# Graph network kernel: gathered pairs tied to the products beside them, the count matrix moved in four pieces a group, 56 edge slots a node

## The chip, the cores and the metric

The kernel runs on one core of one Trainium2 chip. The metric is device microseconds of one execution; the time before is the median of three runs.

## What is computed

A graph has 2500 nodes with 256 features and 80000 edges, sorted by their target. The features are normalized and passed through a relu, then go through three edge convolutions and a last linear layer over all four feature sets:

```python
def _edge_conv(x, src, dst, W, b):
    xi = x[dst]
    xj = x[src]
    m = jnp.concatenate([xi, xj - xi], axis=-1) @ W + b
    s = jax.ops.segment_sum(m, dst, num_segments=N)
    cnt = jax.ops.segment_sum(jnp.ones((dst.shape[0],), m.dtype), dst, num_segments=N)
    return s / jnp.maximum(cnt, 1.0)[:, None]
...
for W, b in ((W0, b0), (W1, b1), (W2, b2)):
    h = jax.nn.relu(_edge_conv(h, src, dst, W, b))
    xs.append(h)
return jnp.concatenate(xs, axis=-1) @ Wf + bf
```

The result is added to the input `x`.

## The kernel before

The sum over edges is a product with a count matrix: entry (m, n) says how many edges go from node m to node n. All nodes are cut into 20 tiles of 128. Of each layer the kernel first makes z, the node features times the lower half of the weights (`nodes_split`, L754, 20 tiles; layer 0 has its own steps for it), keeps it in SBUF as a high and a low part (`zh`, `zl`), and stores it to DRAM as `z_dram`. In `layer` (L934) it then multiplies z with the count matrix: for each of 20 source tiles four products (two column halves, high and low), and four products of the features with the upper half of the weights (L953). Each such step of the generator is a unit; there are 24 in a group.

The targets are worked off in groups of columns. The last 2388 nodes are in windows of 6 nodes; 80 windows (480 columns) make a group, so there are five groups, the last with 78 windows (468 columns). Two tiles `a` hold two groups of the count matrix at a time. In layer 0 the matrix of group g + 1 is built from the edges (`build`, L838) while group g is multiplied, and `finish` (L850) stores the built group to DRAM (`a_dram`) with one transfer. Layer 1 runs through the groups from 4 down to 0 and layer 2 from 0 up to 4; the two groups that lie in SBUF at a layer's start are used first, and the other three are loaded by `load_a` (L856), each with one transfer, when a tile comes free (L1089).

The first 112 nodes (FEW) are not in the count matrix. Each has EDGES slots for edges (L330), and row numbers in `who` say which row of `z_dram` each slot wants; unused slots point to a row of zeros. For layer 0 `gather` (L874) issues one indirect transfer a slot on POOL, the transfers of slots 8 to 59 adding into eight partial sums in SBUF, which `add_sums` (L882) folds on DVE at the layer's end. `layer_few` (L923) multiplies them in; the next layer's `nodes_split` stands behind it on PE. For layers 1 and 2 `gather_pairs` (L904) gathers two slots at a time into one of four rooms, and DVE adds a pair to a running sum before its room is used again. It starts with four pairs and then does a step at units 1, 5, 9, 13, 17 and 21 of each group (the loop at L1056). `final` (L778) adds the features' share of the last linear layer, tile by tile, at the start of each group.

Wrappers whose name ends in "o" (PEo, DVEo, POOLo, ACTo, SPo; the helper is L280) fix an instruction behind everything written earlier for its engine. Instructions on plain PE, ACT and SP may be placed earlier by the scheduler when their inputs are ready. The stores of `z_dram` in `nodes_split` (L764) are on SPo; the loads and stores of the count matrix are on plain SP. A count of nodes with more edges than slots (`shares`, with `most`) sets a flag that makes a general kernel run afterwards.

Of the kernel before, what the change touches and what calls it, by code (L numbers as in the profile page):

```python
# [8 lines left out]
F32 = mybir.dt.float32  # L9
# [302 lines left out]
def by_windows(ctx: ExitStack, tc: tile.TileContext, x, src, dst, Ws, bs, Wf, bf, out, missing):  # L312
    nc = tc.nc
    PE, DVE, ACT, POOL, SP = nc.tensor, nc.vector, nc.scalar, nc.gpsimd, nc.sync
    PEo, DVEo, POOLo, ACTo, SPo = (InOrder(tc, e) for e in (PE, DVE, POOL, ACT, SP))
    P = 128
    N, D = x.shape
    E = src.shape[0]
    NT = (N + P - 1) // P
# [7 lines left out]
    S = 8  # L327
    CAP = CH * P
    FEW = 112
    EDGES = 60  # L330
    SUMS = 8
    PAIRS = 4
    NW = (N - FEW) // W
# [14 lines left out]
    NG = len(GWS)  # L348
# [20 lines left out]
    def bank():  # L369
        return ps[-1].tile([P, 512], F32, name="bank")  # L370
# [3 lines left out]
    hT = const.tile([P, DC, NP], F32, name="hT")  # L374
    zh = const.tile([P, NT, D], F32R, name="zh")
    zl = const.tile([P, NT, D], F32R, name="zl")
# [19 lines left out]
    z_dram = [dram.tile([NP, D], F32, name=f"z_dram{l}") for l in range(L)]  # L396
    who = const.tile([P, EDGES], I32, name="who")
    sums = const.tile([P, SUMS, D], F32, name="sums")
# [4 lines left out]
    a_dram = [dram.tile([P, NT, n * W], F32, name=f"a_dram{g}") for g, n in enumerate(GWS)]  # L403
# [25 lines left out]
    ws = [None] * L  # L429
# [6 lines left out]
    def load_wt(l, queue=SP):  # L436
        queue.dma_start(ws[l][0], Ws[l][0:D, :].rearrange("(c p) d -> p c d", p=P))
# [41 lines left out]
    POOL.memset(mine[:IN_LAST], 1.0)  # L479
    POOL.memset(most, float(EDGES))  # L480
    POOL.memset(most[:IN_LAST], float(CAP))
# [104 lines left out]
    def few_edges():  # L586

        es, ed = edges[WG - 1]
        own = pp.tile([P, EDGES], I32, name="own")
        POOLo.tensor_scalar(who, es[:, :EDGES], -NONE, None, op0=OP.add)  # L590
        POOLo.tensor_scalar(own, away[:, WG - 1, :EDGES], 0.0, None, op0=OP.is_equal)
        POOLo.tensor_tensor(who, who, own, op=OP.mult)
# [161 lines left out]
    def nodes_split(l, t, zf):  # L754
        pz = bank()
        for c in range(DC):
            PE.matmul(pz[:, :D], hT[:, c, t * P:(t + 1) * P], ws[l][1][:, c, :],  # L757
                      start=(c == 0), stop=(c == DC - 1))
        sc = share[:, t:t + 1]
        if t == NT - 1:  # L760
            DVEo.scalar_tensor_tensor(zf, pz[:, :D], sc, brow[:, l % 2, :], op0=OP.mult, op1=OP.add)
        else:
            ACT.activation(zf, pz[:, :D], AF.Copy, scale=sc)
        SPo.dma_start(z_dram[l][t * P:(t + 1) * P, :], zf)  # L764
        DVEo.tensor_copy(zh[:, t, :], zf)
        DVEo.tensor_sub(zl[:, t, :], zf, zh[:, t, :].bitcast(F32))
# [22 lines left out]
    def group_of(g):  # L789
        return FEW + sum(GWS[:g]) * W, GWS[g] * W  # L790

    def touched(g):
        c0, n = group_of(g)
        return [t for t in range(NT) if (t + 1) * P > c0 and t * P < c0 + n]

    def new_a(g):

        n = group_of(g)[1]
        a = apools[g % 2].tile([P, NT * GS], F32R, name="a")
        return a[:, :NT * n].rearrange("p (t n) -> p t n", n=n)  # L800
# [49 lines left out]
    def finish(g, a):  # L850
        c0, n = group_of(g)
        ACTo.copy(a[PAD:PAD + 1, NT - 1, :n], cnt[PAD:PAD + 1, c0:c0 + n])
        SP.dma_start(a_dram[g], a.bitcast(F32))
        yield

    def load_a(g):  # L856
        a = new_a(g)
        SP.dma_start(a.bitcast(F32), a_dram[g])
        return a

    def by_count(g):
# [12 lines left out]
    def gather(l):  # L874

        for e in range(EDGES):
            POOLo.indirect_dma_start(
# [9 lines left out]
    def room():  # L887

        return hot.tile([P, BW * CH, P], BF16, name="one_m", bufs=AHEAD).rearrange(
            "p k m -> p (k m)").bitcast(F32).rearrange("p (i d) -> p i d", i=2)  # L890

    def rooms(l):

        for _ in range(AHEAD):
            two = room()
            yield two[:, 0, :]
            yield two[:, 1, :]
        for i in range(SUMS):
            yield sums[:, i, :]
        for _ in range(AHEAD):  # L900
            yield hot.tile([P, BW * CH, NB], BF16, name="one_n", bufs=AHEAD).rearrange(
                "p k m -> p (k m)")[:, :2 * D].bitcast(F32)

    def gather_pairs(l):  # L904

        got = []
        for k in range(EDGES // 2 + PAIRS):
            if k >= PAIRS:
                if k == PAIRS + 1:
                    DVEo.tensor_add(sums[:, :2, :], got[0], got[1])  # L910
                elif k > PAIRS:
                    DVEo.tensor_add(sums[:, :2, :], sums[:, :2, :], got[k - PAIRS])
            if k < EDGES // 2:
                two = room()
                got.append(two)
                for i in range(2):
                    POOLo.indirect_dma_start(
                        out=two[:, i, :], out_offset=None, in_=z_dram[l][:, :],
                        in_offset=bass.IndirectOffsetOnAxis(ap=who[:, 2 * k + i:2 * k + i + 1], axis=0))
            if k >= PAIRS - 1:  # L920
                yield

    def layer_few(l):  # L923
        pa = ps_agg.tile([P, DC, 512], F32, name="pa")
        for o in range(DC):
            for c in range(DC):
                PEo.matmul(pa[:, o, :FEW], ws[l][0][:, c, o * P:(o + 1) * P], hT[:, c, :FEW],
                           start=(c == 0), stop=False)
            for z in (zh, zl):
                PEo.matmul(pa[:, o, :FEW], z[:, NT - 1, o * P:(o + 1) * P], cnt_few, start=False, stop=False)  # L930
            PEo.matmul(pa[:, o, :FEW], sums[:, 0, o * P:(o + 1) * P], only, start=False, stop=True)
        ACTo.activation(hT[:, :, :FEW], pa[:, :, :FEW], AF.Relu)

    def layer(l, g, a, own, PE=PE, ACT=ACT):  # L934

        c0, n = group_of(g)
        pa = ps_agg.tile([P, DC, 512], F32, name="pa")
        ways = [(o, c) for o in range(DC) for c in range(DC)]
        units = [(0, k) for k in range(NT)]
        for i, u in enumerate(own):  # L940
            units.insert(u + i, (1, i))
        last = {}
        for kind, i in units:
            last.update({o: (kind, i, o) for o in (range(DC) if kind == 0 else ways[i][:1])})
        for kind, i in units:
            if kind == 0:
                for o in range(DC):
                    for z in (zh, zl):
                        PE.matmul(pa[:, o, :n], z[:, i, o * P:(o + 1) * P], a[:, i, :n],  # L949
                                  start=(i == 0 and z is zh), stop=(z is zl and last[o] == (kind, i, o)))  # L950
            else:
                o, c = ways[i]
                PE.matmul(pa[:, o, :n], ws[l][0][:, c, o * P:(o + 1) * P], hT[:, c, c0:c0 + n],  # L953
                          start=False, stop=(last[o] == (kind, i, o)))
            yield
        ACT.activation(hT[:, :, c0:c0 + n], pa[:, :, :n], AF.Relu)  # L956

# [7 lines left out]
    a = new_a(0)  # L965
# [55 lines left out]
    for g in range(NG):  # L1021
# [26 lines left out]
        if g + 1 < NG:  # L1048
            run(finish(g + 1, a1))
            held, a = a, a1  # L1050
# [4 lines left out]
    tiles = {NG - 1: a, NG - 2: held}  # L1055
    for l in range(1, L):  # L1056
        groups = list(range(NG))
        if l % 2:
            groups.reverse()


        last = [t for t in touched(groups[0]) if t]
        for t, zf in zip([t for t in range(1, NT) if t not in last] + last + [0], rooms(l)):
            nodes_split(l, t, zf)
        few = gather_pairs(l)
        next(few)
        if l + 1 < L:
            load_b(l + 1)
            load_wb(l + 1)
            load_wt(l + 1)  # L1070
        finished = []
        for j, g in enumerate(groups):
            now = [t for t in touched(g) if t not in finished]
            for t in now:
                final(l, t)
            finished += now
            rest = add_rest(now) if l == 1 else None
            if j == NG - 1:
                load_wf(l + 1)
            for u, _ in enumerate(layer(l, g, tiles[g], LATE)):  # L1080
                if u % 4 == 1:
                    next(few, None)
                if rest and u in (1, NT):
                    next(rest, None)
            if j == 1 and l + 1 < L:
                DVEo.tensor_sub(ws[l + 1][0], ws[l + 1][0], ws[l + 1][1])
            if j + 2 < NG:
                del tiles[g]
                tiles[groups[j + 2]] = load_a(groups[j + 2])  # L1089
        run(few)  # L1090
        add_sums(2)
        layer_few(l)
# [41 lines left out]
```

## Time and profile before

| | us |
|---|---|
| median of three runs | 531.79 (531.63 to 532.43) |
| the profiled execution, its own time | 533.3 |
| its span, first to last instruction | 531.6 |
| TensorE products busy in the span | 506.9 |
| POOL busy | 268.9 |
| DVE busy | 264.6 |

PE is TensorE's products, PEld its weight loads, DVE is VectorE, ACT ScalarE, POOL GpSimd and SP the queue that issues most transfers. Times in the views are counted from the first instruction. The profile gives the granted clock of TensorE and, by engine, what ended each wait. "issue" is time in which an engine waited for nothing that the profile shows. Layer 0 ends near 216, layer 1 near 360 and layer 2 near 508.

### The profile page before, as it was taken

The numbers are of one execution on the slowest core, as the hardware profiler recorded it, in microseconds if no ns is written. First come the engines' busy times: TensorE is split into PE (matmuls) and PEld (weight loads), VectorE is DVE, ScalarE is ACT, GpSimd is POOL, SyncE is SP. The second block draws the span as 40 slices with busy tenths as digits, with TensorE's granted clock in tenths as the row PEclk, the third lists the DMA queues.
The fourth block names the chain that finished last, engine by engine and source line by source line (L and its number), as shares of the span: only waits on it lengthen the run. The fifth ranks groups of instructions, "written<-read, shape, count | busy, mean of one in ns | idle before, by whom it ended". The sixth has DMA issues, their size and how long they took to land.

```text
span 531.6 us, 7489 instructions
## 1 busy us (share of the span) xinstructions
PE 506.9 (95%) x2875; PEld 414.1 (78%) x2875; DVE 264.6 (50%) x556; ACT 136.0 (26%) x310; POOL 268.9 (51%) x243
## 2 busy tenths in 40 slices
PE   8999999999999993999899999999996999999995
PEld 4898887888787882888587878878883878787884
DVE  7999888888888501582134140426620313303133
ACT  5676666746443400330000000005200000000000
POOL 3793257888888850007856462720273537354000
PEclk9999999999999998799999999999997999999998
DMA  8238749988968586343499999883334868998323
GB/s 275 82 99 137 142 144 355 391 164 268 222 168 291 82 320 129 98 141 91 107 415 331 234 276 244 114 108 118 110 105 142 351 238 255 193 283 92 30 89 110
DMA packets 37683, 100.29 MB, mean 189 GB/s; under 512 B 4663, under 2 KB 31750, under 8 KB 36230
## 3 DMA queue, kind: packets, MB, share of 16 engines
q0 software_dynamic: 19264, 29.84, 34.8%
q1 hardware_dynamic: 17446, 68.78, 33.4%
q10 hardware_dynamic: 928, 1.11, 0.7%
q8 instruction: 24, 0.39, 0.3%
q14 instruction: 21, 0.17, 0.1%
HBM read 62.21 MB, written 37.50 MB: 188 GB/s over the span
## 4 chain that ended last, share of the span: by engine, by line
PE 66%; POOL 14%; DMA 14%; issue 4%; DVE 1%; ACT 0%; SPq 0%; POOLq 0%; ACTq 0%
PE pa L949 33%; POOL sums L280 14%; PE bank L781 10%; DMA sums<-z_dram,who 10%; PE bank L757 7%; PE pa L953 6%; PE pz L280 6%; PE bank L280 2%; DMA wf<-in_L_gnn_Wf_dram 2%; PE pa L280 1%; DMA z_dram<-zl 1%; DMA z_dram<-zh 1%; DMA dst_i<-in_dst_dram 1%; PE turned L280 1%; DVE sums L280 0%
## 5 line engine op out<-in xcount | busy, mean ns | idle before, releaser
L280 POOL DMA_INDIRECT one_m<-z_dram,who x120 | 121.1, 1009 | 168.8 <-DVE sums L280 53.3
L949 PE MATMUL pa<-a,zh 128*128 128x480 f32 (+1 forms) x400 | 153.9, 385 | 0.3 <-issue 0.3
L949 PE MATMUL pa<-a,zl 128*128 128x480 f32 (+1 forms) x400 | 151.9, 380 | 0.3 <-issue 0.3
L280 POOL DMA_INDIRECT sums<-z_dram,who x60 | 104.2, 1737 | 24.7 <-issue 17.4
L280 DVE TENSOR_TENSOR sums<-sums,one_m 128x512 f32<-128x512 f32 x56 | 38.8, 692 | 103.3 <-DMA one_m<-z_dram,who 99.6
L949 PEld LDWEIGHTS pa<-a,zl 128*128 128x128 f32 x400 | 75.1, 188 | 13.2 <-issue 1.2
L949 PEld LDWEIGHTS pa<-a,zh 128*128 128x128 f32 x400 | 75.1, 188 | 12.8 <-issue 0.5
L280 PE MATMUL pa<-a,zh 128*128 128x480 f32 (+1 forms) x200 | 81.6, 408 | 0.0
L280 DVE TENSOR_TENSOR one_m<-iota_m,key_m 128x1024 bf16<-128x1024 bf16 x100 | 68.8, 688 | 17.6 <-PE bank L280 15.3
L280 PE MATMUL pa<-a,zl 128*128 128x480 f32 (+1 forms) x200 | 75.7, 379 | 0.0
L956 ACT ACTIVATE hT<-pa 128x960 f32<-128x960 f32 (+1 forms) x10 | 9.7, 968 | 243.8 <-PE pa L953 212.1
L280 DVE SCALAR_TENSOR_TENSOR acc<-bank,share,acc 128x256 f32<-128x256 f32 x60 | 28.5, 483 | 79.6 <-PE bank L781 69.0
L280 ACT CAST a<-bank 128x480 fp32r<-128x480 f32 x100 | 51.0, 566 | 59.7 <-PE bank L280 55.1
L280 DVE TENSOR_TENSOR one_n<-iota_n,key_n 128x960 bf16<-128x960 bf16 x100 | 65.3, 653 | 0.0
L781 PE MATMUL bank<-wf,hT 128*128 128x256 f32 x240 | 56.3, 391 | 2.0 <-issue 1.5
L781 PEld LDWEIGHTS bank<-wf,hT 128*128 128x128 f32 x240 | 47.1, 197 | 12.3 <-issue 5.3
L280 PEld LDWEIGHTS <-one_m 128*128 128x128 bf16 x796 | 43.3, 98 | 8.9 <-issue 3.3
L280 PE MATMUL bank<-one_n,one_m 128*128 128x120 bf16 x796 | 49.0, 216 | 0.2 <-DVE one_n L280 0.2
L280 PEld LDWEIGHTS pa<-a,zh 128*128 128x128 f32 x200 | 37.7, 188 | 8.5 <-issue 3.0
L280 PEld LDWEIGHTS pa<-a,zl 128*128 128x128 f32 x200 | 37.6, 188 | 7.0 <-issue 2.1
L953 PE MATMUL pa<-hT,wt 128*128 128x480 f32 (+1 forms) x80 | 35.4, 573 | 4.6 <-issue 4.5
L757 PE MATMUL bank<-wb,hT 128*128 128x256 f32 x160 | 36.0, 388 | 0.0
(145 smaller groups left out, 417.2 us busy)
## 6 DMA issues: line engine op xcount, KB each, us to landing
a<-a_dram SPq DMA_DIRECT2D x5, 4800.0 KB
a_dram<-a SPq DMA_DIRECT2D x4, 4800.0 KB
a_dram<-a SPq DMA_DIRECT2D x1, 4680.0 KB
a<-a_dram SPq DMA_DIRECT2D x1, 4680.0 KB
out_dram<-acc SPq DMA_DIRECT2D x19, 128.0 KB
z_dram<-one_m SPq DMA_DIRECT2D x16, 128.0 KB
z_dram<-sums SPq DMA_DIRECT2D x16, 128.0 KB
acc<-in_x_dram POOLq DMA_DIRECT2D x4, 512.0 KB
```

Of the source, the lines that this page charges most:

```text
L280: return self.tc.keep_in_program_order(call(*args, **kwargs))
L757: PE.matmul(pz[:, :D], hT[:, c, t * P:(t + 1) * P], ws[l][1][:, c, :], start=(c == 0), stop=(c == DC - 1))
L781: PE.matmul(po[:, :D], hT[:, c, t * P:(t + 1) * P], wfs[l][:, c, :], start=(c == 0), stop=(c == DC - 1))
L949: PE.matmul(pa[:, o, :n], z[:, i, o * P:(o + 1) * P], a[:, i, :n], start=(i == 0 and z is zh), stop=(z is zl and last[o] == (kind, i, o)))
L953: PE.matmul(pa[:, o, :n], ws[l][0][:, c, o * P:(o + 1) * P], hT[:, c, c0:c0 + n], start=False, stop=(last[o] == (kind, i, o)))
L956: ACT.activation(hT[:, :, c0:c0 + n], pa[:, :, :n], AF.Relu)
```

## The change

The number of edge slots falls from 60 to 56. The stores and loads of the count matrix are made in four transfers of five source tiles each. The store of the last group leaves `finish` and is written after the node products of layer 1 (the second of the three layers, `l == 1`), on plain SP. `layer` remembers its latest product in `unit`, and from the fifth pair on the first gather of each pair waits for the product that was the latest when it was written.

```diff
-    EDGES = 60
+    EDGES = 56
...
     def finish(g, a):
         c0, n = group_of(g)
         ACTo.copy(a[PAD:PAD + 1, NT - 1, :n], cnt[PAD:PAD + 1, c0:c0 + n])
-        SP.dma_start(a_dram[g], a.bitcast(F32))
+        if g + 1 < NG:
+            store_a(g, a)
         yield
+
+    def store_a(g, a):
+        for t in range(0, NT, 5):
+            SP.dma_start(a_dram[g][:, t:t + 5, :], a[:, t:t + 5, :].bitcast(F32))
 
     def load_a(g):
         a = new_a(g)
-        SP.dma_start(a.bitcast(F32), a_dram[g])
+        for t in range(0, NT, 5):
+            SP.dma_start(a[:, t:t + 5, :].bitcast(F32), a_dram[g][:, t:t + 5, :])
         return a
...
                 for i in range(2):
-                    POOLo.indirect_dma_start(
+                    d = POOLo.indirect_dma_start(
                         out=two[:, i, :], out_offset=None, in_=z_dram[l][:, :],
                         in_offset=bass.IndirectOffsetOnAxis(ap=who[:, 2 * k + i:2 * k + i + 1], axis=0))
+                    if k >= PAIRS and i == 0:
+
+                        tc.add_manual_dep(d.ins, unit[0].ins.name, mybir.DependencyInfo(
+                            mybir.DependencyClass.Sync, mybir.DependencyReason.DATA), reason="spread over the layer")
...
+    unit = [None]
...
-                        PE.matmul(pa[:, o, :n], z[:, i, o * P:(o + 1) * P], a[:, i, :n],
-                                  start=(i == 0 and z is zh), stop=(z is zl and last[o] == (kind, i, o)))
+                        unit[0] = PE.matmul(pa[:, o, :n], z[:, i, o * P:(o + 1) * P], a[:, i, :n],
+                                            start=(i == 0 and z is zh),
+                                            stop=(z is zl and last[o] == (kind, i, o)))
             else:
                 o, c = ways[i]
-                PE.matmul(pa[:, o, :n], ws[l][0][:, c, o * P:(o + 1) * P], hT[:, c, c0:c0 + n],
-                          start=False, stop=(last[o] == (kind, i, o)))
+                unit[0] = PE.matmul(pa[:, o, :n], ws[l][0][:, c, o * P:(o + 1) * P], hT[:, c, c0:c0 + n],
+                                    start=False, stop=(last[o] == (kind, i, o)))
...
             nodes_split(l, t, zf)
+        if l == 1:
+
+            store_a(NG - 1, tiles[NG - 1])
         few = gather_pairs(l)
```

## The prediction

> **What bounds the kernel now.** I read the page's busy table and its row of granted clock, then the chain of work that ended last, the table of waits, and windows around the places where TensorE (PE) stops.
>
> ```profile
> span 531.6 us, 7489 instructions
> ...
> PE 506.9 (95%) x2875; PEld 414.1 (78%) x2875; DVE 264.6 (50%) x556; ACT 136.0 (26%) x310; POOL 268.9 (51%) x243
> ...
> PEclk9999999999999998799999999999997999999998
> ```
>
> PE is busy for all but 24.7 us. The first dip of the clock is the end of layer 0. The chain there (start, duration, what):
>
> ```profile
> 191.35 0.30 issue
> 191.66 1.54 POOL sums L280
> 193.20 0.30 issue
> 193.50 17.73 DMA sums<-z_dram,who
> ...
> 213.72 2.47 PE pa L280 x10
> 216.19 18.36 PE bank L757 x80
> ...
> 358.14 1.77 PE pa L280 x16
> 359.91 17.28 PE bank L757 x80
> ```
>
> It leaves PE and runs through the 60 accumulating gathers: POOL issues one every 1.84 us (1.54 + 0.30), the last lands 17.73 us after its issue, VectorE (DVE) folds the eight partial sums from 211.26 to 213.67, and only then PE ends the product of the first 112 nodes. The last two lines are the same two stages a layer later, undisturbed. The waits agree:
>
> ```profile
> DVE sums L280 <- DMA sums<-z_dram,who: 25.6, 1, 25.6
> PE pa L280 <- DVE sums L280: 9.1, 1, 9.1
> ```
>
> Windows there (busy time of PE, PEld, DVE, ACT, POOL; granted clock, DMA share, GB/s):
>
> ```profile
> 176.00:180.00 4.00, 4.00 (x38) 3.46 (x37) 3.27 (x10) 1.57 (x3) 3.39 (x3) 1.00 0.62 84
> 192.00:196.00 4.00, 4.00 (x21) 3.56 (x19) 0.00 (x0) 0.00 (x0) 2.74 (x2) 1.00 0.92 375
> 208.00:212.00 4.00, 0.00 (x0) 0.00 (x0) 0.74 (x1) 0.00 (x0) 0.00 (x0) 0.50 0.43 51
> ```
>
> From 189 to 204 the DMA engines carry the store of the last group (375 GB/s) over the gathers; then PE idles and its clock halves. The second dip, in the first group of layer 2, is another kind of stop:
>
> ```profile
> 403.50 0.56 PE L953 MATMUL pa<-hT,wt 128*128 128x480 f32 x1 [0.84 <-issue]
> 404.92 0.56 PE L953 MATMUL pa<-hT,wt 128*128 128x480 f32 x1 [0.85 <-issue]
> ```
>
> PE waits for no engine, yet takes an instruction only each 0.70 us (weight load, product, weight load). From 399.08 to the next group's first product at 414.23 pass 15.15 us; the group after needs 3.22 + 3.45 = 6.67 for the same work, so 8.5 us are lost. A short one in layer 1 (255.87 to 264.56, 8.69 against 3.14 + 3.45) loses 2.1.
>
> **What the Trainium skill says.** "DMA: Bandwidth & Descriptors", Queues, rings and completion order: an engine round-robins between the queues it has work for and changes only after a whole packet. The trace agrees: during that store an engine alternates one packet of 37,440 bytes (1.40 us) with one gathered row of 1,024 bytes (0.10 us). The same page, Anatomy of one DMA: a semaphore wait is held on the issuing sequencer, so a gated gather holds up POOL, not the DMA engines; no gate is in this trace. "TensorE: Matmul & The Clock Gate", Part 1: an idle array falls to half clock and must be busy a while to come back. Here the clock is 0.50 for 10.2 us, from 208.0. "Runtime: NRT & Kernel Launch", Instruction fetch mechanics, describes instructions streamed in 16 KiB blocks, mostly hidden; 24 packets of 16,384 bytes are in the trace, but neither page nor trace gives the cause of the 0.70 us pace.
>
> **Part by part.**
>
> *56 edges.* Four gathers fewer in layer 0: 4 x 1.84 = 7.4 us of POOL, so the last one is issued at about 186.1, not 193.5. In layers 1 and 2 two pairs fewer each, beside the products: nothing on the path. The largest number of edges into one of the first 112 nodes in these inputs is 47, so the flag for the general kernel stays down.
>
> *Four transfers a group.* 11 transfers (5 stores, 6 loads) become 44. An issue costs SP 0.32, so 3 x 0.32 = about 1 us more per group. Behind a store stand the weight loads for layer 1 (76.4 to 80.7, needed at 216), behind a load only the next one: nothing. Packets should fall from 38,400 to 9,600 bytes, 1.42 / 4 = 0.355 us. With a row between (0.10), 32 packets an engine take 32 x 0.455 = 14.6 us (before, 8 x 1.5 = 12), in which 32 rows an engine, four gathers, pass instead of one. Counting the packets of the gathers' queue against their issues, gather 56 lagged 17.6 us before. Now: a lag of about 3 us ahead of the store at 155; POOL issues about 7 in 14.6 us and 4 pass, so 3 x 1.75 us are added (1.75 is the drain per gather without a store); by 186 some 6.7 is left. For PE's own loads: 14.6 us, up to 20 with more gather packets and 2.2 of start, against 24 between need and issue (a group is 17.57 + 3.22 + 3.45), and the first quarter comes early. Cost zero; with the cover gone a load would show as a wait of L949.
>
> *The last store moved.* Its four issues pass the 20 stores of `z_dram` on SP, in program order; on POOL nothing is passed. But it is an unpinned SP transfer, and such ones float: the layer-2 `wt` load, written after those 20 stores, was issued at 215.37, ahead of the first at 218.47. So it may still start near 185. I cost both places. If it moves, gather 56 lands at 186.1 + 6.7 = 193. If not, some 2.7 gathers are left when its packets start (189), at 8 rounds x 0.455 = 3.6 us each: 199. With the 2.4 us fold the sums are ready at 195 or 201, before 204.6. After a move it fills 235 to 250, where the DMA share was 0.3 to 0.4, and the first gathers of layer 1 land later; they have four groups to catch up.
>
> So the wait goes: 213.72 - 204.58 = 9.14 us. PE stays warm, so the two stages after it take their layer-2 times: 2.47 - 1.77 = 0.70 and 18.36 - 17.28 = 1.08. Sum **10.9 us**. Next late is PE itself.
>
> *Gates.* 24 pairs in each of two layers wait for a product; a semaphore instruction is 0.05 us on POOL's queue. Behind a gate stand later gathers and the additions of `x` (L768), which only the next layer reads. In the first group the gates are open before POOL arrives: a unit takes 17.58 / 20 = 0.88 us, so pair 4 opens at 383.3 in layer 2, where the ninth gather went at 390.4 anyway, and pair 9 near 400 to 402, against 402.9. Later groups had 12 gathers each before and have 12 now. The last gate is unit 21 of the fourth of five groups, about 480; with layer 2's largest lag, 9.9 us, the pair is there at 491, and PE wants the sum at 506. Cost zero, and, as the first burst keeps its pace, no gain that I can work out either. For the two stalls I take no change; the bounds are all 10.6 us gone, or as much again.
>
> From the profiled execution: 533.3 us (span 531.6) less 10.9. The median is 1.5 us under that execution, so the forecast from it is 531.8 - 10.9 = **520.9**, and 519.5 to 522.5 if only the small terms are off.
>
> **Rivals.**
> - *The slow pace of PE goes too* (0.22). For: both stalls come after some 17 gathers in a row, and end about when POOL pauses; the gates and the earlier start shift that. Against: the first burst is unchanged. Both gone 510.3, the long one alone 512.4.
> - *The wait goes only in part* (0.10): packets do not shrink and the store floats. Gather 56 was through at 203.7; with the fold 206.3, so 1.8 us stay: 522.7.
> - *The slow pace spreads* (0.05, slower). If gathers beside a product cause it, spreading them through every group gives each of the eight groups undisturbed so far in layers 1 and 2 a stall. At the short one's price 8 x 2.1 = 16.8: 520.9 + 16.8 = 537.7; at the long one's 589. It decides once the new stalls pass 10.9 us, two long ones.
> - *No effect* (0.03): the end of layer 0 waits for something behind the sums that the trace hides: about 531.8.
>
> **How the numbers follow.** Forecast 0.60, rivals 0.22, 0.10, 0.05, 0.03. Low end 510.0 takes in both stalls gone, high end 523.5 the part-wait; some 0.1 is outside. About 0.2% (1.1 us) is what a measurement of this kernel can tell from no change: faster 0.92, same 0.03, slower 0.05.
>
> **What would show it.** Right: no wait of PE on `sums` near 204, clock 1.00 there, `wt` and `bank` stages of 1.8 and 17.3 us. The chain passes from the last group's products straight to L757. Packets near 9,600 bytes. The forecast is wrong if PE waits in L949 for a load, if DVE's fold ends after 204.6, if the layers 1 and 2 show new "issue" stops, or none at all.

## The result, and the profile after

| | us |
|---|---|
| before, median of 4 runs | 532.11 (531.63 to 535.16) |
| after, median of 4 runs | 511.65 (510.90 to 512.34) |
| ratio, 95% interval | 0.9604 (0.9565 to 0.9642) |
| the profiled execution after, its own time | 510.9 (span 509.1) |

The kernel is faster by 20.5 us; the forecast of 520.9 was 9.2 us too high. The edits shift the line numbers of `layer`: its products with the count matrix are L949 before and L961 after, those of the features L953 and L966. The page after, its span, TensorE's (PE's) busy time and the granted clock:

```profile
span 509.1 us, 7543 instructions
...
PE 498.3 (98%) x2875; PEld 410.4 (81%) x2875; DVE 262.4 (52%) x552; ACT 135.9 (27%) x310; POOL 250.2 (49%) x231
...
PEclk9999999999999999999999999999999999999999
```

Both dips of the clock are gone, and the same 2875 products are busy for 8.6 us less. The chain of work that ended last (start, duration, what) shows the end of layer 0:

```profile
187.23 15.51 DMA sums<-z_dram,who
203.12 1.24 DVE sums L280
...
205.59 1.37 PE pa L280 x10
206.95 17.28 PE bank L757 x80
```

The last gather is issued 6.3 us earlier than before and lands 8.5 us earlier. The fold of the partial sums still ends after PE needs them, though by little, as the table of waits says (total, times, longest):

```profile
DVE sums L280 <- DMA sums<-z_dram,who: 18.2, 1, 18.2
...
PE pa L280 <- DVE sums L280: 1.8, 1, 1.8
```

The windows at 192 and 204 (busy time of PE, PEld, DVE, ACT, POOL; granted clock, DMA share, GB/s) give the reason: the store of the last group (374 GB/s; its packets of 9,360 bytes run from 185.8 to 202.1) still lies over the last gathers, so it has not moved.

```profile
192.00:196.00 4.00, 4.00 (x21) 3.55 (x20) 0.00 (x0) 0.00 (x0) 0.00 (x0) 1.00 1.05 374
204.00:208.00 4.00, 2.41 (x16) 2.29 (x17) 2.06 (x4) 0.70 (x3) 0.00 (x0) 1.00 0.09 13
```

The slow pace at the end of the first group of layer 2 is nearly gone. On the chain, the first two of the eight products of L966 are followed by the other six after a gap of 0.14 us:

```profile
368.68 17.41 PE pa L961 x80
386.09 0.91 PE pa L966 x2
387.14 2.68 PE pa L966 x6
389.82 3.45 PE bank L781 x16
393.28 17.33 PE pa L961 x80
```

In layer 1 about half of the slow stretch is left, among the products of `final`:

```profile
248.65 1.08 PE bank L781 x5
249.72 0.44 issue
250.17 0.59 PE bank L781 x2
250.76 0.81 issue
251.57 1.24 PE bank L781 x5
```

Read between the same marks of both chains, the 22.5 us of span are:

| stretch | before | after | gained |
|---|---|---|---|
| to the first product of `final` (L781) in layer 1 | 234.55 | 224.24 | 10.31 |
| layer 1, first group (to the next group's products) | 30.01 | 28.57 | 1.44 |
| layer 1, the other four groups | 93.58 | 92.50 | 1.08 |
| layer 2, node products | 19.05 | 19.05 | 0 |
| layer 2, first group | 37.04 | 28.92 | 8.12 |
| layer 2, the other four groups | 91.98 | 91.21 | 0.77 |
| last stage | 25.39 | 24.61 | 0.78 |

The forecast was about the first row alone (10.9). Layer 2's first group gives most of the rest. Nor was it foreseen that 80 products of 480 columns take 17.31 us and no longer 17.57; the last group's, of 468 columns, stay at 16.95.

### The profile page after: what moved, and what is told of

Same layout as the page of the kernel before. It is cut to its first block, busy times and chain, and to the rows that moved or that the text cites. A ratio compares the mean times of both kernels' runs of the same rounds, so it can differ in the third digit from the quotient of the medians.

```text
span 509.1 us, 7543 instructions
## 1 busy us (share of the span) xinstructions
PE 498.3 (98%) x2875; PEld 410.4 (81%) x2875; DVE 262.4 (52%) x552; ACT 135.9 (27%) x310; POOL 250.2 (49%) x231
## 4 chain that ended last, share of the span: by engine, by line
PE 67%; POOL 19%; DMA 8%; issue 4%; DVE 1%; ACT 0%; DVEq 0%; POOLq 0%; SPq 0%; ACTq 0%
PE pa L961 34%; POOL sums L280 19%; PE bank L781 10%; PE bank L757 7%; PE pa L966 6%; PE pz L280 6%; DMA sums<-z_dram,who 3%; PE bank L280 2%; DMA wf<-in_L_gnn_Wf_dram 2%; DMA z_dram<-zl 1%; DMA z_dram<-zh 1%; PE pa L280 1%; DMA dst_i<-in_dst_dram 1%; PE turned L280 1%; DVE sums L280 0%
## 5 line engine op out<-in xcount | busy, mean ns | idle before, releaser
L280 POOL DMA_INDIRECT one_m<-z_dram,who x112 | 111.0, 991 | 153.2 <-DVE acc L280 40.5
L961 PE MATMUL pa<-a,zh 128*128 128x480 f32 (+1 forms) x400 | 152.8, 382 | 0.0
L961 PE MATMUL pa<-a,zl 128*128 128x480 f32 (+1 forms) x400 | 151.4, 378 | 0.0
L280 POOL DMA_INDIRECT sums<-z_dram,who x56 | 95.7, 1710 | 23.8 <-issue 16.8
L280 DVE TENSOR_TENSOR sums<-sums,one_m 128x512 f32<-128x512 f32 x52 | 36.0, 692 | 106.1 <-DMA one_m<-z_dram,who 104.2
L961 PEld LDWEIGHTS pa<-a,zl 128*128 128x128 f32 x400 | 75.1, 188 | 11.3
L961 PEld LDWEIGHTS pa<-a,zh 128*128 128x128 f32 x400 | 75.1, 188 | 11.0
L781 PE MATMUL bank<-wf,hT 128*128 128x256 f32 x240 | 54.0, 379 | 1.8 <-issue 1.3
L781 PEld LDWEIGHTS bank<-wf,hT 128*128 128x128 f32 x240 | 45.5, 190 | 11.4 <-issue 5.1
L757 PE MATMUL bank<-wb,hT 128*128 128x256 f32 x160 | 34.9, 379 | 0.0
L966 PE MATMUL pa<-hT,wt 128*128 128x480 f32 (+1 forms) x80 | 34.0, 565 | 0.1
```

Of the source, the lines that this page charges most:

```text
L280: return self.tc.keep_in_program_order(call(*args, **kwargs))
L781: PE.matmul(po[:, :D], hT[:, c, t * P:(t + 1) * P], wfs[l][:, c, :], start=(c == 0), stop=(c == DC - 1))
L961: unit[0] = PE.matmul(pa[:, o, :n], z[:, i, o * P:(o + 1) * P], a[:, i, :n], start=(i == 0 and z is zh), stop=(z is zl and last[o] == (kin ...
L966: unit[0] = PE.matmul(pa[:, o, :n], ws[l][0][:, c, o * P:(o + 1) * P], hT[:, c, c0:c0 + n], start=False, stop=(last[o] == (kind, i, o)))
```

## Experiments

The theory: at the end of layer 0 the gathers end earlier (fewer slots, smaller packets); the slow pace of PE comes from a long row of gathers on POOL, which the waits break up. The rivals: the packets of the count matrix or the number of slots cause the slow pace; or it belongs to PE's own place in the program and the waits matter in another way.

**One part alone.** Three kernels are the one before with one part added, and one is the one after with the waits taken out. All four ran on one chip, where the kernel before took 534.5 us (median of 15).

`e1_gates`: only the waits are added (60 slots, one transfer a group).

```diff
+                    if k >= PAIRS and i == 0:
+                        tc.add_manual_dep(d.ins, unit[0].ins.name, ...)
```

Expected: 

> The kernel before with the gates alone (60 slots, one transfer a group, the last store where it was). Theory 'gates': the pause that they give POOL in the first group of layers 1 and 2 ends the slow pace of PE there, so the two stops shrink from 10.6 us to about 1.3 and the time falls by some 9.3 us, to about 522.5; the wait for the sums at the end of layer 0 stays at 9.1. Rival 'packets' or 'slots': gates do nothing, about 531.8, and the stop near 400 is still 8.5 us.

Measured: 524.59 us, ratio 0.9801 (0.9742 to 0.9860). The wait at the end of layer 0 stays (sums ready at 211.08), the products stay at 17.57, and the slow pace shrinks: on the chain of layer 2's first group (378.00 to 404.19, so 26.19 us where the kernel before took 32.72) it is a gap of 1.2 us and a small one:

```profile
378.00 16.70 PE pa L958 x76
394.70 1.19 issue
395.89 0.38 PE pa L958
396.27 0.33 issue
396.60 0.92 PE pa L958 x3
397.51 3.22 PE pa L963 x8
```

By the traces the two first groups, from their L781 to the next group's products, are together 7.9 us shorter than in the kernel before (28.64 and 30.51 for 30.01 and 37.04). The spans differ by 10.1; the other 2.1 us lie ahead of layer 1, where the sums are ready 2.6 us earlier, and the edit, which touches layers 1 and 2 alone, does not explain them.

`e2_pieces`: only the four transfers a group.

```diff
-        SP.dma_start(a_dram[g], a.bitcast(F32))
+        for t in range(0, NT, 5):
+            SP.dma_start(a_dram[g][:, t:t + 5, :], a[:, t:t + 5, :].bitcast(F32))
```

Expected: 

> The kernel before with four transfers a group alone. Theory 'packets': the shorter packets end the slow pace of PE, 9.3 us less, and the last of the 60 gathers lands earlier by about 2 us: about 520.5. Rival 'gates': both stops of PE stay, and only the 2 us at the end of layer 0 come: about 530.

Measured: 534.21 us, ratio 0.9992 (0.9963 to 1.0021): no change. The last gather lands 1.9 us earlier (209.30, not 211.23), but PE still waits for it, and both slow stretches are there (layer 2's first group takes 36.83 us from its L781 to the next group).

`e3_slots`: only `EDGES = 56`.

Expected: 

> The kernel before with 56 slots alone. All theories: the last gather is issued 7.4 us earlier and was through at 203.7 in the trace of before, so the wait falls to about 2 us and the clock stays up: 9 us less, 523. If the smaller list of rows, which shifts what lies behind it in SBUF by 32 bytes, also makes the products with 480 columns faster, another 2 us: 521. Rival 'slots': the slow pace goes with them too, about 511.5.

Measured: 527.41 us, ratio 0.9849 (0.9777 to 0.9920). Both slow stretches stay. The products of 480 columns take 17.31 us, so that gain comes with the slots. PE doesn't wait for the sums at all: their last gather is issued at 182.27, ahead of the last store (188.29), and the fold is through at 195.78. The time is still above the 521 to 523 us expected, among other things because PE itself comes later: near 84 it waits 1.0 us for VectorE's `one_n`, the clock dips, and PE reaches the next node products at 209.47, not at 206.95 as after the whole change.

`e4_no_gates`: the whole change without the waits.

Expected: 

> The changed kernel without its gates. Theory 'gates': both stops come back whole, 9.3 us more than the changed kernel, about 521. Rivals 'packets' and 'slots': no change, about 511.7.

Measured: 525.84 us, ratio 0.9827 (0.9767 to 0.9887). Both stretches are back, in layer 1 from 251.7 to 255 and in layer 2 among the last products of the count matrix. The timeline of PE (start, duration, what, idle before):

```profile
387.76 0.38 PE L961 MATMUL pa<-a,zh 128*128 128x480 f32 x1 [1.75 <-issue]
389.87 0.56 PE L961 MATMUL pa<-a,zl 128*128 128x480 f32 x1 [1.74 <-issue]
391.97 0.56 PE L961 MATMUL pa<-a,zh 128*128 128x480 f32 x1 [1.54 <-issue]
```

That group's stretch takes 39.36 us (365.43 to 404.79) against 28.92 with the waits. What follows from the four: the waits alone shorten the slow stretches, in the traces by 7.9 us on the kernel before and by 11.0 on the whole change; packets and slots don't. (The medians differ by 9.9 and by 14.2, the second of two chips.) That refutes the two rivals that blame the packets or the slots.

**What else belongs to the change.** Four kernels ran on a second chip (before: 532.76 us, median of 11).

`e5_whole`: the change, with one transfer a group again.

Expected: 

> The changed kernel, but with one transfer a group again (waits of the gathers on products and 56 slots stay). If the four pieces do nothing, or even cost the first gather its early start, the end of layer 0 loses its 1.64 us wait of PE for the sums, as in the kernel with 56 slots alone, and the time is 508 to 512 us, 0.955 to 0.962 of before. If the small packets are worth something to the gathers, the first-group waits or the loads, it is 513 us or more, and a wait of PE for the sums or for a load of a is in the trace.

Measured: 513.37 us, ratio 0.9619 (0.9581 to 0.9657). The last gather is issued at 184.24 and lands 20.25 us later, at 204.49, where with four pieces it lands at 202.74. So small packets do help the gathers, by 1.75 us, although with them the first gather starts later (76.28 us, here 71.23: the first pieces of group 0's store go ahead of the last store of `z_dram`). Of the two branches the second came: the wait of PE for the sums grew, from 1.8 us to 2.8.

`e6_moved`: the change, with the last store on the pinned SP queue (`store_a` now takes the queue as an argument).

```diff
-            store_a(NG - 1, tiles[NG - 1])
+            store_a(NG - 1, tiles[NG - 1], SPo)
```

Expected: 

> The changed kernel, with the last store on the pinned SP queue, so that it stands behind the stores of layer 1's node products and really leaves layer 0. If the rest of the wait at the end of layer 0 (1.64 us of PE on the sums, and the colder clock after it) is that store's doing, it goes: 508.5 to 510.5 us. If the store only moves the crowding to the first gathers of layer 1, a new slow stretch of PE or a later last gather there gives the gain back: 511 to 514 us.

Measured: 507.59 us, ratio 0.9515 (0.9481 to 0.9548), 4.1 us below the change itself (whose ratio, beside a kernel before of 532.11, is 0.9604). The chain stays on PE at the end of layer 0:

```profile
184.13 21.22 PE pa L280 x100
205.35 17.28 PE bank L757 x80
```

and the store's traffic is gone from 192 and lies after the node products of layer 1:

```profile
192.00:196.00 4.00, 4.00 (x20) 3.56 (x19) 0.56 (x1) 0.00 (x0) 0.00 (x0) 1.00 0.51 46
...
236.00:242.00 6.00, 6.00 (x30) 5.33 (x29) 1.97 (x3) 0.00 (x0) 1.67 (x3) 1.00 0.71 265
```

VectorE starts its fold at 195.44, not at 203.12. In layer 1 the store holds POOL up after eight gathers (one at 236.4, the next at 241.4), and the slow stretch there is gone as well: the first group takes 26.99 us, not 28.57. In the traces these 1.6 us and as much at the end of layer 0 are all that the two kernels differ by (spans of 506.0 and 509.1). So the change as written does not move the store: on plain SP its four transfers stand in the built program where the single one stood.

`e7_place`: the change, with `who` allocated 60 columns wide and used 56 wide.

```diff
-    who = const.tile([P, EDGES], I32, name="who")
+    who = const.tile([P, 60], I32, name="who")[:, :EDGES]
```

Expected: 

> The changed kernel, but the tile who is allocated 60 columns wide and used 56 wide, so that all tiles behind it lie where they lay before, 32 bytes higher. If the quicker products (80 of 480 columns in 17.31 us, not 17.57) come from that place in SBUF, they are back at 17.57 and the time rises by 8 to 12 groups x 0.26 = 2 to 3 us, to 513.5 to 515 us. If they come from the smaller number of gathers, they stay at 17.31 and the time at 511.6 us.

Measured: 515.27 us, ratio 0.9658 (0.9621 to 0.9695). The quicker products are gone:

```profile
278.13 17.57 PE pa L961 x80
295.71 3.22 PE pa L966 x8
```

So it is the place in SBUF that counts. With 56 columns `who` is smaller, and the tiles behind it lie 32 bytes lower (in the built program the first count matrix starts at byte 151,200 of a partition, not 151,232). 0.26 us in each of the eight full groups of layers 1 and 2 are 2.1 us. They are not the whole distance of the two medians, which are of different chips.

`e8_late`: the change without the later waits, the first gather of layers 1 and 2 tied to unit 17 of the first group.

Expected: 

> The changed kernel without the waits of the later gathers, and with the first gather of layers 1 and 2 made to wait for the product of unit 17 of the first group, some 12 to 14 us later than now; after that the gathers run back to back. If a long row of gathers on POOL is what makes PE slow, the slow stretch of 0.70 us an instruction comes that much later, in the second group: near 262 to 268 in layer 1 and 398 to 402 in layer 2, and the time stays near the 525.8 us of the kernel without waits. If it belongs to PE's own place in the program (its instructions number some 3540 and 4740 in every trace so far), it comes at the end of the first group as before, near 251 and 386, or not at all when it takes both: then the time is 511 to 515 us.

Measured: 522.62 us, ratio 0.9793 (0.9747 to 0.9838). Neither form of the expectation came: there is no slow stretch in the first group nor in the second. The time is lost elsewhere, since the late gathers end after the products of their layer:

```profile
PE pa L280 <- DVE sums L280: 11.1, 3, 5.9
```

PE runs through the same instructions as in the other kernels without a stop, so the stretch does not belong to its place in the program. The gathers, tied to nothing but the first product, come here in shorter rows: in layer 1 fourteen with two loads of `x` between them, in layer 2 eight (396.56 to 405.48), then, after a pause of 3.4 us, fourteen (409.79 to 427.85). That no row is longer than fourteen agrees with the long row as the cause, but does not show it: in the kernel after PE slowed, if little, after a row of fourteen.

**A pause instead of a wait.** The last four kernels were meant to part a long row from the tie to PE. They ran on a third chip, and there the kernel before takes 520.18 us (519.68 to 522.46, 9 runs).

`e9_pause`: no waits; POOL has other work after twelve gathers (the four multiplications took 1.72 us, not 4).

```diff
+            if k == 6:
+                for i in range(4):
+                    POOLo.tensor_scalar(sums[:, 4 + i, :], sums[:, 4 + i, :], 1.0, 0.0, op0=OP.mult, op1=OP.add)
```

Expected: 

> The changed kernel without the waits of the gathers on products; in layers 1 and 2 POOL multiplies four rows of sums that nobody reads any more by one after the twelfth gather, which takes it some 4 us (0.93 us each). If a row of 14 to 18 gathers without a pause is what makes PE slow, any pause ends it: no stop of PE over 1 us in the first groups of layers 1 and 2, and 511 to 514 us. If only the tie to PE's products helps, the slow stretches come as in the kernel without waits (from about 252 and 386) and the time is about 525.8 us. If the number of gathers since the layer's start counts and not the row, the slow stretch starts after the 14th to 18th gather all the same, about 4 us later.

Measured: 509.21 us, ratio 0.9785 (0.9765 to 0.9806), no slow stretch. `e12_pause1`, the same with one multiplication:

Expected: 

> As the kernel with POOL's pause and without waits, but with one multiplication, a pause of about 1 us instead of 4. If any break of the row is enough, 511 to 514 us. If what POOL has handed out must first drain (a gather lands 2.4 us after its issue here), 1 us is not enough and the slow stretches come back in full or in part: 518 to 526 us.

Measured: 509.80 us, ratio 0.9801 (0.9776 to 0.9827), no slow stretch. `e11_moved_pause`, the four multiplications in the kernel whose store moves, with its waits:

Expected: 

> The kernel with the last store really moved, waits of the gathers kept, and POOL's pause of about 4 us after the twelfth gather of layers 1 and 2. What is left of the slow stretch there is 0.9 us in layer 2 and nothing in layer 1. If a row of gathers is the cause, that goes too: 506.5 to 507.2 us. If not, 507.6 us; if the late gathers make PE wait for sums at a layer's end, 509 us or more.

Measured: 506.75 us, ratio 0.9739 (0.9718 to 0.9759), the fastest of all; no slow stretch. `e10_moved_whole`, the store moved and one transfer a group:

Expected: 

> The kernel with the last store really moved behind layer 1's node products, but with one transfer a group. If the four pieces are worth nothing once that store is away, it is at the 507.6 us of the same with four pieces, within 1 us. If small packets help the gathers or the loads elsewhere, it is 509 us or more; if the first pieces' passing of the z store costs something, it is 506.5 us or less.

Measured: 507.96 us, ratio 0.9760 (0.9737 to 0.9783). With the store away from layer 0 the whole transfers cost nothing visible there: the node products of layer 1 start at 204.95, in `e11_moved_pause` with four pieces at 204.99. But this trace spoils the test of the pause. POOL's timeline in layer 2 shows twenty gathers in a row from 364.53, 1.25 us apart, the waits all open when POOL came to them. The last two of that row and the next gather, after a pause:

```profile
387.19 0.95 POOL L280 DMA_INDIRECT one_m<-z_dram,who  x1 [0.30 <-PE bank L781]
388.45 0.94 POOL L280 DMA_INDIRECT one_m<-z_dram,who  x1 [0.30 <-issue]
391.78 0.94 POOL L280 DMA_INDIRECT one_m<-z_dram,who  x1 [2.39 <-PE pa L959]
```

The kernel before had twenty in a row too (380.22 to 404.19), and PE crawled from the 16th on. Here the chain runs through the group with no stop:

```profile
365.79 17.33 PE pa L959 x80
383.12 3.22 PE pa L964 x8
386.34 3.45 PE bank L781 x16
389.79 17.31 PE pa L959 x80
```

`e9_pause` has such a row too, behind its pause (383.60 to 409.21), and no stop. So on this chip twenty in a row did not slow PE, and the two pauses show nothing of the cause. The 520.18 us of the kernel before fit that: they are 11.6 us under the 531.79 of the runs shown first, and the two stretches there had cost 11.4. No trace of the kernel before was taken on this chip, so this last step is argued, not shown.

**When PE's signals arrive.** The views show when a product ends; the traces also hold the time at which its semaphore, the signal to other engines, was raised. (Some of these records are missing; signals and products are paired in order.) In the kernel after, the gather at 387.44 in layer 2 waits for a product that ended at 380.80, and the signal of that product was raised at 387.18. In layer 1 the signals of five products that ended between 243.80 and 249.51 were all raised between 251.63 and 251.90. The kernel before has signals 9.4 and 9.5 us late at its two stretches, and every other trace of the first three groups of runs has some in layer 1 or 2. In the four traces of the third chip every signal of PE from 222 to 300 and from 360 to 415 was raised within 0.02 us of its product's end.

The held signals came through soon after the last rows of the gathers had landed (landed at 386.41, 250.44 and, before, 406.68; raised at 387.18, 251.63 and 408.59), and PE was back at its pace within 0.2 us of that. So the long row, the late signals and the slow pace come together, and all three end together. Which of them brings on which is not shown: in `e7_place` a signal of layer 2 was 6.6 us late and PE did not stop, and in `e4_no_gates` PE slowed at 385.6 with no signal due from 369.74 to 396.43.

## Why the prediction came out as it did

From execution to execution the forecast was 533.3 - 10.9 = 522.4, and the profile after is 510.9, so 11.5 us more were gained. The rest of the miss in the medians (9.2) is the profiled executions' distance from them, +1.5 before and -0.75 after.

- **The wait at the end of layer 0: right in place, 0.6 us too large in size.** 10.31 for 10.92. PE's wait fell from 9.14 us to 1.75 and did not vanish, while PE came to it 0.75 us sooner; the stage behind it ran warm, 17.28, as forecast, and the one of ten products took 1.37, less than the 1.77 that I had taken. "sums are ready at 195 or 201" failed for the place where the store stays: they were ready at 205.54. The first gather started 5.3 us later, which I had not priced, and the last was issued at 187.2, not 186.1. It landed 15.5 us after that, not 13: the store's packets began at 185.8, not 189, with the rows of 4.9 gathers (628 of 1,024 bytes, 128 to a gather) still to come, not 2.7. The other branch, the store really moved, held in its conclusion: in `e6_moved` the sums are ready at 197.85, not 195, and PE does not wait.
- **The last store: the doubt was right.** It floats. The size I gave to the move was nothing beyond the wait; `e6_moved` shows 4.1 us between the medians, of different chips, and 3.1 between the traces: half of it the end of layer 0, half the slow stretch of layer 1.
- **Packets: right.** DMA queue lines, packets, megabytes and share, before:

```profile
q1 hardware_dynamic: 17446, 68.78, 33.4%
```

  and after:

```profile
q1 hardware_dynamic: 22198, 68.78, 36.7%
```

  The same bytes in more packets: one of 9,600 bytes took 0.375 us. The gathers' rows passed between them as forecast: over the last store some 54 rows and 54 packets end in each 1.5 us, where before it was 16 and 16. No load showed as a wait of PE. By itself this part is worth nothing that the medians show (`e2_pieces`); in the change it brings the last gather home 1.75 us sooner (`e5_whole`).
- **Gates: the step that failed.** "Cost zero, and, as the first burst keeps its pace, no gain that I can work out either. For the two stalls I take no change." The cost was indeed nothing, and the burst was not unchanged: after 14 gathers in layer 2 POOL stood still for 3.6 us from issue to issue, where my timing had every gate of the first group open. I had taken a gate to open when its product ends; its signal came 6.4 us later.

```profile
383.82 0.94 POOL L280 DMA_INDIRECT one_m<-z_dram,who  x1 [0.30 <-issue]
387.44 0.94 POOL L280 DMA_INDIRECT one_m<-z_dram,who  x1 [2.67 <-PE pa L961]
```

  PE's gap on the chain, 387.00 to 387.14, lies within that pause. The two first groups gained 9.56 us, and `e1_gates` and `e4_no_gates` show that the waits are what gained them. Of the two rivals on the slow pace, "goes too" (510.3 to 512.4) is in the main what happened, for its reason "the gates", though 1.6 us are left of the short stretch and 0.6 of the long one; "spreads" is refuted, no other group shows a stop. The short stretch was also under-priced: 8.69 us was set against a whole round of `final`, 3.45, but the group behind it has only 12 of those 16 products, 2.59 us (`e6_moved`), so it cost 3.0 us, not 2.1.
- **What was luck.** The time lies near the low end of the stated range, which reached so far down for this rival alone. The forecast's own mechanism gives about half of the gain.
- **Not seen at all: the products' pace.** 1.08 + 0.77 us in the undisturbed groups, and some 0.2 in the first of layer 2, from a table that became smaller (`e7_place`). The last stage gave another 0.78: it takes 25.2 to 25.5 us in the five kernels with one transfer a group and 24.6 to 25.0 in those with four (but for `e8_late`, whose sums are late there); why was not looked for.

The terms: 9.56 + 1.85 + 0.78, less 0.6, are 11.6, beside the 11.5 to be explained.

What stays open is the mechanism of the slow pace. Shown: with the change 9.2 of its 11.4 us are gone, and it is the waits that take them away; it is not bound to PE's instructions; with a row of 20 gathers it came in the kernel before and did not come in two kernels on another chip. That the row causes it, where the signals come late, is consistent with `e8_late` and with `e6_moved` in layer 1, but was not isolated. Nor does any run tell why the signals are late on some chips, or whether the recording of the trace has a part in it. The Trainium skill, "Runtime: NRT & Kernel Launch", Instruction fetch mechanics, has each engine stream its instructions in 16 KiB blocks; 24 such packets are in every trace that I counted, those with slow stretches too, each of 0.9 to 1.9 us. In the trace before none starts within a slow stretch (the nearest at 252.3 and 290.4, 375.6 and 409.6), and they tell no cause.

## What to carry to other kernels

When an engine stops in a profile with no wait behind it, don't price that stop at "unchanged": look for what another engine does at that very time, and give a change that breaks its rhythm a weight of its own, up to the whole stop. A wait opens when the signal is raised, and here that was up to 9.5 us after the product had ended. A transfer that is moved in the source may stay where it was in the program if its queue is not pinned; look at where its traffic lies in the trace afterwards. Compare kernels on one chip, since a stop such as this one can be there on one chip and, it seems, not on another.

## What the hardware showed that I had not expected

- PE can be held to one instruction each 0.70 us (at times 0.80 or 1.40) with no wait of its own and no crowded DMA in sight: the DMA share was 0.33 in the kernel before from 399 to 407. Signals of its finished products were up to 9.5 us late at the time.
- This differs between chips. In three groups of runs the kernel before took 532.1 to 534.5 us, and every trace of theirs has late signals; in the fourth it took 520.2 us, and there signals stood within 0.02 us of their products and twenty gathers in a row slowed nothing (`e9_pause`, `e10_moved_whole`).
- 32 bytes of place in SBUF change products of 480 columns by 1.5%: 17.31 us or 17.57 for eighty, while those of 468 columns take 16.95 in either place.
- A transfer cut into four started earlier: its first piece went ahead of a store that the whole had followed, and held the gathers up by 5.3 us.
